# A perceiver layer on one core: the first context group turned block by block while x is normalised, and the last two places run one token tile after the other

## The chip, the core and the metric

The kernel runs on one core of a Trainium2 chip. The metric is the device time of one execution in microseconds, as the median of several runs. TensorE (PE in the profile, with its weight loads as PEld) multiplies and transposes; it takes its operands from SBUF and writes into the eight banks of PSUM, each 128 partitions by 512 float32 numbers. VectorE (DVE) and ScalarE (ACT) read those banks and write SBUF. GpSimd (POOL) has a small part. Transfers from and to memory are issued by the queue of SyncE (SP) or of ScalarE and run on sixteen shared DMA engines. All data are float32.

## The reference

A batch of one: 256 tokens `x` of 512 channels, and a context of 25088 rows of 512 channels. Three residual parts follow one another.

```python
x = x + xattn(layernorm(x), ctx, ctx)   # qp = q Wq + bq, kp = k Wk + bk (128 wide), vp = v Wv + bv
                                        # sigmoid(qp kp^T / sqrt(128)) @ vp, no softmax
x = x + attn(layernorm(x))              # 16 heads of 64, one shared key and value head, causal softmax,
                                        # projection, layernorm of the result
x = x + ffn(layernorm(x))               # 64 experts of width 256, the best 8 for each token,
                                        # and a shared expert of width 1024 behind a sigmoid gate
```

## The kernel before

**The cross attention** takes most of the time. The 25088 rows are cut into 49 groups of 512 rows (four blocks of 128). For a group the kernel needs the context turned (channels on the partitions, `cT`), the keys (`keys`, line 339: four chunks of 128 channels summed into one PSUM bank, then a DVE copy with the bias, `kT`), the scores (`scores`, line 360: two banks, each of two blocks by 256 queries, then ACT's sigmoid into `zT`), and the sum of context rows weighted by the scores (`values`, line 432, in seven products instead of eight, from sums and differences that DVE prepares in `query_sums` and `context_sums`). Those products stay in four PSUM banks (`xacc`, pool `pacc`, tag `acc`) over all groups. From the third group on the context is turned by DVE from a second load of it (`quarters`); the first two groups are turned by TensorE (`turn_by_pe`, line 320: chunk after chunk, four transposes into one bank, and a copy of the bank to SBUF by DVE or ACT in turn).

**PSUM.** Four banks are the accumulators. The other four are shared by everything else in this stage: `bank` (line 80) gives every fourth request the one bank called `apart`, and the other requests one of three under the tag `one`. A request has to wait until the bank's last user has been copied out. After the cross attention the accumulators make place for two pairs of banks (`banks`, line 580).

**The start.** bk and bq are loaded by ACT's queue. SP's queue issues, in this order, the two tiles of x (256 KB each), wqT, the first context group in four parts of 256 KB, the plain key weights (256 KB), the second group (1 MB in one), the key weights in another order (four parts), and the quarters of the third group. TensorE first runs idle matmuls (`keep_warm(4)`, line 457). DVE and ACT normalise x tile by tile (`layernorm`: `bn_stats`, `bn_aggr`, a square root on ACT, a reciprocal and one scaling). TensorE then transposes x into `xnT` (`transposed`, line 300, copied by DVE), turns group 0, makes the queries (`pq`, then `qT` with its bias), the keys of group 0, turns group 1, and enters the loop over the groups. Instructions inside `in_turn` keep the program's order on their engine; the others are placed by the framework's own scheduler. All the matmuls of this stage and nearly all of DVE's work are pinned so.

**The end.** In the expert part, eight places are run whole, one expert each: `gate_up` makes the hidden tile `hT` for all 256 tokens, `down` (line 977) multiplies it with the down weights for each of the two token tiles and adds the weighted result to `y`. `run` (line 1000) lets `gate_up` of the next place go ahead of `down` of the one before. Seven more experts with few tokens are computed in between in 32-row quarters; their results in `of_sb` are spread over the tokens by `few_spread` (line 1246: for each token tile three products, added to `y`). It stands behind the `down` of the last but one place. After the last `down` both token tiles of `y` are stored by SP (`store`, line 1275). Then a count read from memory decides whether further experts remain, which here is a branch not taken.

Of the kernel before, what the change touches and what calls it, by code (L numbers as in the profile page):

```python
# [9 lines left out]
F32 = mybir.dt.float32  # L10
AF = mybir.ActivationFunctionType
ALU = mybir.AluOpType
AX = mybir.AxisListType

P = 128
# [6 lines left out]
def tile_perceiver_layer(  # L22
# [25 lines left out]
    nc = tc.nc  # L48

    T, D = x.shape  # L50
    S = context.shape[0]
    QK = wqT.shape[1]
# [6 lines left out]
    NT = T // P  # L59
    ND = D // P  # L60
    NI = I // P
    J = 4
# [11 lines left out]
    cpool = cross.enter_context(tc.tile_pool(name="cpool", bufs=2))  # L74
# [15 lines left out]
    pacc = cross.enter_context(tc.tile_pool(name="pacc", bufs=4, space=bass.MemoryType.PSUM))  # L90

    def load(name, shape, src, pool=const):
        t = pool.tile(shape, F32, tag=name, name=name, bufs=1)
        nc.sync.dma_start(t, src)
        return t

    def rows(src):
        return src.rearrange("(c p) f -> p c f", p=P)  # L100
# [25 lines left out]


    BY_PE = 2
    bk_sb = const.tile([QK, 1], F32, tag="bk", name="bk")
    nc.scalar.dma_start(bk_sb, bk)  # L130
    bq_sb = const.tile([QK, 1], F32, tag="bq", name="bq")
    nc.scalar.dma_start(bq_sb, bq)
    x_sb = act.tile([P, NT, D], F32, tag="x", name="x_sb")
    for t in range(NT):
        nc.sync.dma_start(x_sb[:, t, :], x[t * P : (t + 1) * P, :])
    wqT_sb = load("wqT", [P, ND, QK], rows(wqT))
    load_context(0, parts=J)
    wk_plain_sb = load("wk_plain", [P, ND, QK], rows(wkT), cpool)
    load_context(1)
    wkT_sb = const.tile([P, ND, QK], F32, tag="wkT", name="wkT_sb")  # L140
    for a in range(NA):
# [52 lines left out]
    ident = const.tile([P, P], F32, tag="ident", name="ident")  # L194
# [41 lines left out]
    def keep_warm(n):  # L236
        pi = bank("pi")
        for _ in range(n):
            nc.tensor.matmul(pi, lhsT=idle_sb[:, 0:P], rhs=idle_sb, start=True, stop=True)
# [20 lines left out]
    def layernorm(dst, src, nm, twice=False):  # L260

        mean, sd, rs = moments(src, nm, twice)
        in_turn(nc.vector.reciprocal(rs, sd))
        in_turn(nc.vector.tensor_scalar(dst, src, mean, rs, ALU.subtract, ALU.mult))
# [32 lines left out]
                    )  # L297
                )

    def transposed(dst, src, nm):  # L300

        for c in range(ND):
            pt = bank(f"pt_{nm}_{c}")
            for t in range(NT):
                nc.tensor.transpose(
                    pt[:, t * P : (t + 1) * P], src[:, t, c * P : (c + 1) * P], ident
                )
            nc.vector.tensor_copy(dst[:, c, :], pt[:, :T])


    turned_tiles = {}

# [4 lines left out]
        in_turn(nc.vector.transpose(cT, q.rearrange("p b (c r) -> p c b r", r=R)))  # L317
        turned_tiles[g] = cT

    def turn_by_pe(g):  # L320

        cT = cpool.tile([P, ND, J * P // R, R], F32, tag="cT", name=f"cT_{g}")
        ct = ctx_tiles[g]
        for c in range(ND):
            pt = bank(f"ptc_{g}_{c}")
            for j in range(J):
                in_turn(
                    nc.tensor.transpose(
                        pt[:, j * P : (j + 1) * P], ct[:, j, c * P : (c + 1) * P], ident
                    )  # L330
                )
            to = cT[:, c, :, :].rearrange("p b r -> p (b r)")
            if c % 2:
                nc.scalar.copy(to, pt)
            else:
                in_turn(nc.vector.tensor_copy(to, pt))
        turned_tiles[g] = cT

    def keys(g):

        cT = turned_tiles.pop(g)
        pk = bank(f"pk_{g}")
        w = wk_plain_sb if g < BY_PE else wkT_sb
        for c in range(ND):
            in_turn(
                nc.tensor.matmul(  # L346
                    pk,
                    lhsT=w[:, c, :],
                    rhs=cT[:, c, :, :].rearrange("p b r -> p (b r)"),
                    start=(c == 0),  # L350
                    stop=(c == ND - 1),
                )
            )
        kT = cpool.tile([QK, J * P], F32, tag="kT", name=f"kT_{g}")
        in_turn(nc.vector.tensor_scalar(kT, pk, bk_sb, None, ALU.add))  # L355
        return kT
# [38 lines left out]
    NP = J // 2  # L395
    HD = D // 2
    product = {}
    for i, names in enumerate((("00", "01"), ("2", "3"), ("1",), ("4", "11"))):
        held = pacc.tile([P, 512], F32, tag="acc", name=f"xacc_{i}")
        for k, nm in enumerate(names):  # L400
            product[nm] = held[:, k * HD : (k + 1) * HD]
    sums, channel_sums = {}, {}

    def z_of(zT, i, b):
# [49 lines left out]
                    )  # L454
                )

    keep_warm(4)
    xn = work.tile([P, NT, D], F32, tag="tok", name="xn")
    for t in range(NT):
        layernorm(xn[:, t, :], x_sb[:, t, :], f"x{t}")  # L460
    xnT = work.tile([P, ND, T], F32, tag="tokT", name="xnT")
    transposed(xnT, xn, "xn")
    turn_by_pe(0)
    pq = bank("pq")
    for c in range(ND):
        in_turn(
            nc.tensor.matmul(
                pq[:, :T],
                lhsT=wqT_sb[:, c, :],
                rhs=xnT[:, c, :],  # L470
                start=(c == 0),
                stop=(c == ND - 1),
            )
        )
    qT = cpool.tile([QK, T], F32, tag="qT", name="qT", bufs=1)
    in_turn(nc.vector.tensor_scalar(qT, pq[:, :T], bq_sb, None, ALU.add))
# [103 lines left out]
    def banks(name):  # L580
        return pairs.tile([P, 2, 512], F32, tag="two", name=name)
# [392 lines left out]

    y = late.tile([P, NT, D], F32, tag="y", name="y")

    def down(n, hT):
        _, dn = weights.pop(n)
        nm = f"{n[0]}{n[1]}"
        for t in range(NT):  # L980
            pd = banks(f"pd_{nm}_{t}")[:, 0, :]
            for f in range(NI):
                nc.tensor.matmul(  # L983
                    pd,
                    lhsT=hT[:, f, t * P : (t + 1) * P],
                    rhs=dn[:, f, :],
                    start=(f == 0),
                    stop=(f == NI - 1),
                )
            w = wsh[:, t, :] if n[0] == "s" else wso[:, t, n[1] : n[1] + 1]  # L990
            if n == ("s", 0):
                nc.vector.scalar_tensor_tensor(
                    y[:, t, :], pd, w, x2[:, t, :], ALU.mult, ALU.add
                )
            else:
                nc.vector.scalar_tensor_tensor(
                    y[:, t, :], pd, w, y[:, t, :], ALU.mult, ALU.add
                )

    def run(names, between):  # L1000

        pending = None
        for i, n in enumerate(names):
            hT = gate_up(n, first if n == ("s", 0) else None)
            if pending is not None:
                down(*pending)
            pending = (n, hT)
            if i in between:
                between[i]()
        down(*pending)  # L1010
# [232 lines left out]
                )  # L1243
        nc.scalar.copy(of_sb[:, r, :], po)

    def few_spread():
        for t in range(NT):
            pd = banks(f"pd_few_{t}")[:, 0, :]
            for r in range(NR):
# [7 lines left out]
            nc.vector.tensor_add(y[:, t, :], pd, y[:, t, :])  # L1257

    def places(lo, hi, also=()):
# [10 lines left out]
        run(  # L1270
            [("e", k) for k in range(lo, hi)],
            {i: (lambda fs=fs: [f() for f in fs]) for i, fs in between.items()},
        )

    def store():
        for t in range(NT):
            nc.sync.dma_start(out[t * P : (t + 1) * P, :], y[:, t, :])

    def remaining(lo):

# [3 lines left out]
        with tc.If(n_left > lo):  # L1284
# [93 lines left out]
```

## Time and profile before

| | us |
|---|---|
| median of three runs (797.99 to 798.13) | 798.07 |
| profiled execution, its own time | 798.27 |
| its span in the profile | 796.4 |
| TensorE busy within the span | 784.4 |
| first transpose of x starts / second tile's six go on | 7.87 / 8.39 |
| first matmul of the queries | 11.04 |
| first matmul of the scores of group 0 | 18.02 |
| first matmul of the keys of group 1 | 19.74 |
| last matmul done, start of the last sum | 790.02 |
| second half of the output: store issued | 790.8 |

The profile is of one execution. Its times are microseconds from the start of the span; a matmul in float32 is two instructions of TensorE, a transpose one. A line of the timeline gives the start, the time covered, the engine, the line of the program, the operation and its tiles, the count, and in brackets the idle time before it with what ended it. A line of the chain of waits gives start, duration and the work that the end of the span was waiting for.

### The profile page before, as it was taken

How to read it: one execution, taken by the hardware profiler on the slowest of the kernel's cores; microseconds unless marked ns; L12 is line 12 of the kernel's file. 1: busy time of each engine (PE TensorE's matmuls, PEld its weight loads, DVE VectorE, ACT ScalarE, POOL GpSimd, SP SyncE). 2: the span in 40 equal slices, each digit the busy share in tenths (PEclk: the TensorE clock that was granted, in tenths of full speed). 3: DMA queues.
4: the chain of work that ended last, by engine and by line, in shares of the span. 5: the costliest groups of instructions: out<-in, count | busy, mean ns of one | idle time of the engine just before them, and what ended most of it. 6: DMA issues, size and time to landing. Idle time of an engine off the chain costs nothing.

```text
span 796.4 us, 8701 instructions
## 1 busy us (share of the span) xinstructions
PE 784.4 (98%) x3298; PEld 564.5 (71%) x3298; DVE 496.6 (62%) x820; ACT 112.3 (14%) x248; POOL 21.4 (3%) x44
## 2 busy tenths in 40 slices
PE   9999999999999999999999999999999899999996
PEld 5777777777777777777777777777676586776563
DVE  5766776677766776677766776676656563512222
ACT  2111101110011101110011101110245220110110
POOL 1000000000000000000000000000223000000000
PEclk9999999999999999999999999999999999999998
DMA  9967998999887778777887778720510042769400
GB/s 279 257 165 185 258 243 242 244 248 242 200 205 185 174 176 209 191 184 170 197 206 184 174 177 211 193 72 0 196 44 1 1 133 96 252 233 392 163 1 30
DMA packets 150497, 139.59 MB, mean 175 GB/s; under 512 B 7984, under 2 KB 109872, under 8 KB 150448
## 3 DMA queue, kind: packets, MB, share of 16 engines
q1 hardware_dynamic: 150160, 138.96, 67.1%
q8 instruction: 28, 0.46, 0.3%
q14 instruction: 21, 0.17, 0.1%
q10 hardware_dynamic: 288, 0.00, 0.0%
HBM read 138.42 MB, written 0.52 MB: 174 GB/s over the span
## 4 chain that ended last, share of the span: by engine, by line
PE 96%; DVE 2%; ACT 1%; DMA 0%; POOL 0%; issue 0%; ACTq 0%
PE xacc L448 37%; PE pk L346 21%; PE pz L368 11%; PE ph_e L936 7%; PE pd_e L983 3%; PE ph_s L936 3%; PE pd_s L983 2%; PE pa L651 2%; PE ph_few L1205 1%; PE pw L715 1%; PE py L564 1%; PE ps L741 1%; PE ptp L792 1%; PE po_few L1236 1%; PE pf L1182 1%; PE pd_few L1250 1%
## 5 line engine op out<-in xcount | busy, mean ns | idle before, releaser
L346 PE MATMUL pk<-cT,wkT_sb 128*128 128x512 f32 x376 | 169.0, 592 | 0.0
L448 PE MATMUL xacc<-T,S 128*128 128x256 f32 x588 | 134.9, 379 | 0.0
L376 ACT ACTIVATE zT<-pz 128x512 f32<-128x512 f32 x98 | 58.3, 597 | 479.9 <-PE pz L368 479.2
L448 PEld LDWEIGHTS xacc<-T,S 128*128 128x128 f32 x588 | 111.7, 190 | 15.2
L346 PEld LDWEIGHTS pk<-cT,wkT_sb 128*128 128x128 f32 x376 | 71.4, 190 | 69.9 <-issue 67.4
L317 DVE STREAM_TRANSPOSE cT<-quarters 128x2048 f32<-128x2048 f32 x47 | 108.3, 2304 | 0.0
L448 PEld LDWEIGHTS xacc<-ctx,zT 128*128 128x128 f32 x392 | 74.3, 190 | 31.3 <-issue 23.0
L448 PE MATMUL xacc<-ctx,zT 128*128 128x256 f32 x392 | 93.0, 380 | 0.1
L368 PE MATMUL pz<-qT,kT 128*128 128x256 f32 x392 | 92.6, 379 | 0.0
L368 PEld LDWEIGHTS pz<-qT,kT 128*128 128x128 f32 x392 | 74.4, 190 | 10.1
L416 DVE TENSOR_TENSOR S<-zT 128x256 f32<-128x256 f32 x49 | 20.8, 425 | 91.4 <-ACT zT L376 91.4
L355 DVE TENSOR_SCALAR kT<-pk,bk 128x512 f32<-128x512 f32 x49 | 36.8, 751 | 59.8 <-PE pk L346 59.8
L936 PE MATMUL ph_e<-fT,gu 128*128 128x256 f32 x256 | 57.4, 381 | 0.0
L388 DVE TENSOR_TENSOR zsum<-zsum,zT 128x1024 f32<-128x1024 f32 x48 | 56.8, 1184 | 0.0
L936 PEld LDWEIGHTS ph_e<-fT,gu 128*128 128x128 f32 x256 | 48.0, 190 | 10.6 <-issue 2.2
L448 PE MATMUL xacc<-T,zT 128*128 128x256 f32 x196 | 50.3, 379 | 0.0
L448 PE MATMUL xacc<-ctx,S 128*128 128x256 f32 x196 | 50.3, 379 | 0.0
L448 PEld LDWEIGHTS xacc<-T,zT 128*128 128x128 f32 x196 | 37.2, 190 | 5.1
L448 PEld LDWEIGHTS xacc<-ctx,S 128*128 128x128 f32 x196 | 37.2, 190 | 5.1
L427 DVE TENSOR_TENSOR T<-ctx,T 128x512 f32<-128x512 f32 x49 | 33.9, 692 | 1.7
L428 DVE TENSOR_TENSOR T<-ctx 128x512 f32<-128x512 f32 x49 | 33.5, 685 | 0.0
L429 DVE TENSOR_TENSOR T<-T,ctx 128x512 f32<-128x512 f32 x49 | 33.5, 684 | 0.0
(231 smaller groups left out, 611.3 us busy)
## 6 DMA issues: line engine op xcount, KB each, us to landing
ctx<-in_context SPq DMA_DIRECT2D x48, 1024.0 KB, 6.5
quarters<-in_context SPq DMA_DIRECT2D x188, 256.0 KB, 8.4
gu<-in_e_gate_up SPq DMA_DIRECT2D x12, 1024.0 KB, 7.5
dn<-in_e_down SPq DMA_DIRECT2D x11, 512.0 KB, 4.7
gu_s<-in_s_gate_up SPq DMA_DIRECT2D x8, 512.0 KB, 5.9
a_wqT<-in_a_wqT SPq DMA_DIRECT2D x1, 2048.0 KB, 8.8
a_wout<-in_a_woutT SPq DMA_DIRECT2D x1, 2048.0 KB, 9.9
dn_s<-in_s_down SPq DMA_DIRECT2D x4, 512.0 KB, 7.2
```

The source lines that it names most:

```text
L317: in_turn(nc.vector.transpose(cT, q.rearrange("p b (c r) -> p c b r", r=R)))
L346: nc.tensor.matmul(pk, lhsT=w[:, c, :], rhs=cT[:, c, :, :].rearrange("p b r -> p (b r)"), start=(c == 0), stop=(c == ND - 1),)
L355: in_turn(nc.vector.tensor_scalar(kT, pk, bk_sb, None, ALU.add))
L368: nc.tensor.matmul(pz[:, i * T : (i + 1) * T], lhsT=kT[:, j * P : (j + 1) * P], rhs=qT, start=True, stop=True,)
L376: nc.scalar.activation(zT[:, 2 * h : 2 * h + 2, :].rearrange("p j t -> p (j t)"), pz, AF.Sigmoid, scale=1.0 / math.sqrt(QK),)
L388: in_turn(nc.vector.tensor_add(zsum, zsum, zT))
L427: in_turn(nc.vector.tensor_sub(t2, c_of(ct, 1, 1), t1))
L428: in_turn(nc.vector.tensor_sub(t3, c_of(ct, 1, 1), c_of(ct, 0, 1)))
L429: in_turn(nc.vector.tensor_sub(t4, t2, c_of(ct, 1, 0)))
L448: nc.tensor.matmul(product[nm], lhsT=lhs[:, p, :], rhs=rhs[:, p, :], start=(g == 0 and p == 0 and nm in ("00", "2", "1", "4")), stop=(g == ...
L936: nc.tensor.matmul(ph[:, f * T + lo : f * T + hi], lhsT=gu[:, c, col : col + P], rhs=fT[:, c, lo:hi], start=(c == 0), stop=(c == ND - 1),)
L983: nc.tensor.matmul(pd, lhsT=hT[:, f, t * P : (t + 1) * P], rhs=dn[:, f, :], start=(f == 0), stop=(f == NI - 1),)
```

## The change

1. **Loads.** `x`'s two tiles go out on two queues, the first on SP's and the second on ACT's. SP continues with the four blocks of context group 0; ACT's queue takes the plain key weights and then wqT; bk and bq follow on SP behind the context blocks. The rest of the order stays.
2. **x.** Two idle matmul pairs instead of four. The moments of both token tiles are taken first, then both are scaled. The transposes of x go into four shared banks, taken one after the other, and are copied by ACT (even chunks) and DVE (odd chunks) instead of by DVE alone.
3. **Group 0** is turned block by block (each block's four channel chunks go to four banks), into the four accumulator banks, which are handed to the accumulators afterwards (`open_products`). The order on TensorE is blocks 0, 1, 2, x tile 0, block 3, x tile 1. All the copies come after the last block, ACT taking the even chunks and DVE the odd ones.
4. **Queries** are made in the middle of the keys of group 0: chunks 0 and 1 of the keys, the four of the queries, chunks 2 and 3 of the keys. `context_sums(0)` follows the keys instead of coming before them.
5. **Group 1** is turned block by block as well, into the four shared banks.
6. **The end.** `few_spread` and `down` are cut into functions of one token tile. The last two places run, for token tile 0: few-seat spread, last but one `down`, last `down`, store; then the same for token tile 1, whose last `down`, sum and store are in two halves of 256 channels.

```diff
-    def load(name, shape, src, pool=const):
+    def load(name, shape, src, pool=const, queue=nc.sync):
         t = pool.tile(shape, F32, tag=name, name=name, bufs=1)
-        nc.sync.dma_start(t, src)
+        queue.dma_start(t, src)
...
-    bk_sb = const.tile([QK, 1], F32, tag="bk", name="bk")
-    nc.scalar.dma_start(bk_sb, bk)
-    bq_sb = const.tile([QK, 1], F32, tag="bq", name="bq")
-    nc.scalar.dma_start(bq_sb, bq)
     x_sb = act.tile([P, NT, D], F32, tag="x", name="x_sb")
-    for t in range(NT):
-        nc.sync.dma_start(x_sb[:, t, :], x[t * P : (t + 1) * P, :])
-    wqT_sb = load("wqT", [P, ND, QK], rows(wqT))
+    for t, queue in enumerate((nc.sync, nc.scalar)):
+        queue.dma_start(x_sb[:, t, :], x[t * P : (t + 1) * P, :])
     load_context(0, parts=J)
-    wk_plain_sb = load("wk_plain", [P, ND, QK], rows(wkT), cpool)
+    wk_plain_sb = load("wk_plain", [P, ND, QK], rows(wkT), cpool, nc.scalar)
+    wqT_sb = load("wqT", [P, ND, QK], rows(wqT), queue=nc.scalar)
+    bk_sb = load("bk", [QK, 1], bk)
+    bq_sb = load("bq", [QK, 1], bq)
     load_context(1)
...
-    def turn_by_pe(g):
+    def turned_by_pe(g, where):
         cT = cpool.tile([P, ND, J * P // R, R], F32, tag="cT", name=f"cT_{g}")
+        turned_tiles[g] = cT
         ct = ctx_tiles[g]
-        for c in range(ND):
-            pt = bank(f"ptc_{g}_{c}")
-            for j in range(J):
+        pts = [where(f"ptc_{g}_{c}") for c in range(ND)]
+        for j in range(J):
+            for c in range(ND):
                 in_turn(
                     nc.tensor.transpose(
-                        pt[:, j * P : (j + 1) * P], ct[:, j, c * P : (c + 1) * P], ident
+                        pts[c][:, j * P : (j + 1) * P], ct[:, j, c * P : (c + 1) * P], ident
                     )
                 )
+            yield
+        for c in range(ND):
             to = cT[:, c, :, :].rearrange("p b r -> p (b r)")
             if c % 2:
-                nc.scalar.copy(to, pt)
+                in_turn(nc.vector.tensor_copy(to, pts[c]))
             else:
-                in_turn(nc.vector.tensor_copy(to, pt))
-        turned_tiles[g] = cT
-
-    def keys(g):
+                in_turn(nc.scalar.copy(to, pts[c]))
+        yield
+
+    def keys(g, between=None):
...
         for c in range(ND):
+            if between is not None and c == ND // 2:
+                between()
...
-    keep_warm(4)
+    keep_warm(2)
     xn = work.tile([P, NT, D], F32, tag="tok", name="xn")
-    for t in range(NT):
-        layernorm(xn[:, t, :], x_sb[:, t, :], f"x{t}")
+    found = [moments(x_sb[:, t, :], f"x{t}") for t in range(NT)]
+    for t, (mean, sd, rs) in enumerate(found):
+        in_turn(nc.vector.reciprocal(rs, sd))
+        in_turn(nc.vector.tensor_scalar(xn[:, t, :], x_sb[:, t, :], mean, rs, ...))
     xnT = work.tile([P, ND, T], F32, tag="tokT", name="xnT")
-    transposed(xnT, xn, "xn")
-    turn_by_pe(0)
-    pq = bank("pq")
...
+    pxs = [bank(f"pt_xn_{c}") for c in range(ND)]
+
+    def turn_x(t):
+        for c in range(ND):
+            in_turn(nc.tensor.transpose(pxs[c][:, t * P : (t + 1) * P], xn[:, t, c * P : (c + 1) * P], ident))
+
+    blocks = turned_by_pe(0, sum_bank)
+    for j in range(J - 1):
+        next(blocks)
+    turn_x(0)
+    next(blocks)
+    turn_x(1)
+    next(blocks)
+    open_products()
+    for c in range(ND):
+        if c % 2:
+            in_turn(nc.vector.tensor_copy(xnT[:, c, :], pxs[c][:, :T]))
+        else:
+            in_turn(nc.scalar.copy(xnT[:, c, :], pxs[c][:, :T]))
...
+    kT = keys(0, first_queries)
     context_sums(0)
-    kT = keys(0)
-    turn_by_pe(1)
+    for _ in turned_by_pe(1, bank):
+        pass
...
-    def few_spread():
-        for t in range(NT):
-            pd = banks(f"pd_few_{t}")[:, 0, :]
+    def few_spread(t):
+        pd = bank(f"pd_few_{t}")
...
+    def by_tiles(last_but_one, last):
+        for t in range(NT):
+            few_spread(t)
+            down_tile(*last_but_one, t, mark=in_turn)
+            for lo, hi in ((0, D),) if t == 0 else ((0, D // 2), (D // 2, D)):
+                down_tile(*last, t, lo, hi, mark=in_turn)
+                store_tile(t, lo, hi)
+        weights.pop(last_but_one[0])
+        weights.pop(last[0])
...
-            (7, few_spread),
         ],
+        by_tiles,
     )
...
-    store()
```

`sum_bank(name)` takes one bank of the pool `pacc`. `down_tile(n, hT, t, lo, hi, where, mark)` is the body of the old `down` for one token tile and the channels `lo` to `hi`, in a bank of the pairs. `run` hands the last two places to `last_downs`, here `by_tiles`, once the last `gate_up` is issued.

More of the change, by code (lines that the diff above doesn't have):

```diff
@@ L298, in transposed_tile @@
                 )
-    def transposed(dst, src, nm):
-        for c in range(ND):
-            pt = bank(f"pt_{nm}_{c}")
-            for t in range(NT):
[L305 to L308, printed above, removed]
     turned_tiles = {}
@@ L318, in turn @@
         turned_tiles[g] = cT
-    def turn_by_pe(g):
+    def turned_by_pe(g, where):
         cT = cpool.tile([P, ND, J * P // R, R], F32, tag="cT", name=f"cT_{g}")
+        turned_tiles[g] = cT
         ct = ctx_tiles[g]
-        for c in range(ND):
-            pt = bank(f"ptc_{g}_{c}")
-            for j in range(J):
+        pts = [where(f"ptc_{g}_{c}") for c in range(ND)]
+        for j in range(J):
+            for c in range(ND):
                 in_turn(
                     nc.tensor.transpose(
-                        pt[:, j * P : (j + 1) * P], ct[:, j, c * P : (c + 1) * P], ident
+                        pts[c][:, j * P : (j + 1) * P], ct[:, j, c * P : (c + 1) * P], ident
                     )
                 )
+            yield
+        for c in range(ND):
             to = cT[:, c, :, :].rearrange("p b r -> p (b r)")
             if c % 2:
-                nc.scalar.copy(to, pt)
+                in_turn(nc.vector.tensor_copy(to, pts[c]))
             else:
-                in_turn(nc.vector.tensor_copy(to, pt))
-        turned_tiles[g] = cT
-    def keys(g):
+                in_turn(nc.scalar.copy(to, pts[c]))
+        yield
+    def keys(g, between=None):
         cT = turned_tiles.pop(g)
@@ L397, in tile_perceiver_layer, with sum_bank, open_products @@
     product = {}
[L398 to L401, printed above, removed]
+    def sum_bank(name):
+        return pacc.tile([P, 512], F32, tag="acc", name=name)
+    def open_products():
+        for i, names in enumerate((("00", "01"), ("2", "3"), ("1",), ("4", "11"))):
+            held = sum_bank(f"xacc_{i}")
+            for k, nm in enumerate(names):
+                product[nm] = held[:, k * HD : (k + 1) * HD]
     sums, channel_sums = {}, {}
@@ L455, in values @@
                 )
-    keep_warm(4)
+    keep_warm(2)
     xn = work.tile([P, NT, D], F32, tag="tok", name="xn")
-    for t in range(NT):
-        layernorm(xn[:, t, :], x_sb[:, t, :], f"x{t}")
-    xnT = work.tile([P, ND, T], F32, tag="tokT", name="xnT")
-    transposed(xnT, xn, "xn")
-    turn_by_pe(0)
-    pq = bank("pq")
-    for c in range(ND):
-        in_turn(
[L467 to L472, printed above, removed]
-            )
-        )
@@ L475, in tile_perceiver_layer @@
-    qT = cpool.tile([QK, T], F32, tag="qT", name="qT", bufs=1)
-    in_turn(nc.vector.tensor_scalar(qT, pq[:, :T], bq_sb, None, ALU.add))
+    found = [moments(x_sb[:, t, :], f"x{t}") for t in range(NT)]
+    for t, (mean, sd, rs) in enumerate(found):
+        in_turn(nc.vector.reciprocal(rs, sd))
+        in_turn(
+            nc.vector.tensor_scalar(
+                xn[:, t, :], x_sb[:, t, :], mean, rs, ALU.subtract, ALU.mult
+            )
+        )
+    xnT = work.tile([P, ND, T], F32, tag="tokT", name="xnT")
@@ new lines, in tile_perceiver_layer @@
+    pxs = [bank(f"pt_xn_{c}") for c in range(ND)]
+    def turn_x(t):
+        for c in range(ND):
+            in_turn(
+                nc.tensor.transpose(
+                    pxs[c][:, t * P : (t + 1) * P], xn[:, t, c * P : (c + 1) * P], ident
+                )
+            )
+    blocks = turned_by_pe(0, sum_bank)
[11 more added lines that the diff above has]
+            in_turn(nc.scalar.copy(xnT[:, c, :], pxs[c][:, :T]))
@@ new lines, in tile_perceiver_layer, with first_queries @@
+    qT = cpool.tile([QK, T], F32, tag="qT", name="qT", bufs=1)
+    def first_queries():
+        pq = bank("pq")
+        for c in range(ND):
+            in_turn(
+                nc.tensor.matmul(
+                    pq[:, :T],
+                    lhsT=wqT_sb[:, c, :],
+                    rhs=xnT[:, c, :],
+                    start=(c == 0),
+                    stop=(c == ND - 1),
+                )
+            )
+        in_turn(nc.vector.tensor_scalar(qT, pq[:, :T], bq_sb, None, ALU.add))
@@ L975, in tile_perceiver_layer, with down_tile @@
     y = late.tile([P, NT, D], F32, tag="y", name="y")
[L977 to L982, printed above, removed]
+    def down_tile(n, hT, t, lo=0, hi=D, where=None, mark=lambda ins: ins):
+        dn = weights[n][1]
+        nm = f"pd_{n[0]}{n[1]}_{t}_{lo}"
+        pd = where(nm) if where is not None else banks(nm)[:, 0, :]
+        for f in range(NI):
+            mark(
                 nc.tensor.matmul(
-                    pd,
+                    pd[:, lo:hi],
                     lhsT=hT[:, f, t * P : (t + 1) * P],
-                    rhs=dn[:, f, :],
+                    rhs=dn[:, f, lo:hi],
                     start=(f == 0),
@@ L989, in down, with run @@
                 )
[L990 to L1000, printed above, removed]
+            )
+        w = wsh[:, t, :] if n[0] == "s" else wso[:, t, n[1] : n[1] + 1]
+        onto = x2 if n == ("s", 0) else y
+        nc.vector.scalar_tensor_tensor(
+            y[:, t, lo:hi], pd[:, lo:hi], w, onto[:, t, lo:hi], ALU.mult, ALU.add
+        )
+    def down(n, hT):
+        for t in range(NT):
+            down_tile(n, hT, t)
+        weights.pop(n)
+    def run(names, between, last_downs=None):
         pending = None
@@ L1004, in run @@
             hT = gate_up(n, first if n == ("s", 0) else None)
+            if last_downs is not None and i == len(names) - 1:
+                return last_downs(pending, (n, hT))
             if pending is not None:
@@ L1244, in few_down @@
         nc.scalar.copy(of_sb[:, r, :], po)
-    def few_spread():
-        for t in range(NT):
-            pd = banks(f"pd_few_{t}")[:, 0, :]
-            for r in range(NR):
+    def few_spread(t):
+        pd = bank(f"pd_few_{t}")
+        for r in range(NR):
+            in_turn(
                 nc.tensor.matmul(
@@ L1256, in few_spread, with places @@
                 )
-            nc.vector.tensor_add(y[:, t, :], pd, y[:, t, :])
-    def places(lo, hi, also=()):
+            )
+        nc.vector.tensor_add(y[:, t, :], pd, y[:, t, :])
+    def places(lo, hi, also=(), last_downs=None):
         between = {}
@@ L1272, in places, with store_tile @@
             {i: (lambda fs=fs: [f() for f in fs]) for i, fs in between.items()},
+            last_downs,
         )
+    def store_tile(t, lo=0, hi=D):
+        nc.sync.dma_start(out[t * P : (t + 1) * P, lo:hi], y[:, t, lo:hi])
     def store():
         for t in range(NT):
-            nc.sync.dma_start(out[t * P : (t + 1) * P, :], y[:, t, :])
+            store_tile(t)
+    def by_tiles(last_but_one, last):
+        for t in range(NT):
+            few_spread(t)
[5 more added lines that the diff above has]
+        weights.pop(last[0])
     def remaining(lo):
```

## The prediction

> **What bounds the kernel now.** I read the page first: is there one engine that is never idle?
>
> ```profile
> span 796.4 us, 8701 instructions
> PE 784.4 (98%) x3298; PEld 564.5 (71%) x3298; DVE 496.6 (62%) x820; ACT 112.3 (14%) x248; POOL 21.4 (3%) x44
> PE 96%; DVE 2%; ACT 1%; DMA 0%; POOL 0%; issue 0%; ACTq 0%
> ```
>
> TensorE is. So the change can gain only at the two ends, where something else is last, and it loses wherever it opens a hole in TensorE's row. For the front I read the chain of waits in order of time (start us, us, what):
>
> ```profile
> 0.76 3.61 DMA x_sb<-in_x
> ...
> 7.79 0.56 DVE xn L264
> 8.35 0.04 issue
> 8.39 0.88 PE pt_xn L305 x6
> 9.27 1.94 PE ptc L328 x16
> 11.20 1.80 PE pq L467 x8
> 13.00 3.43 PE pk L346 x8
> 16.43 1.75 PE ptc L328 x16
> 18.18 1.73 PE pz L368 x8
> 19.91 3.43 PE pk L346 x8
> ```
>
> Up to 8.39 the chain is x landing and being normalised; from there TensorE runs without a hole. By the timeline's starts the blocks begin at 11.04 (queries), 16.27 (second transposes), 18.02 (scores) and 19.74 (second keys); queries with first keys take 16.27 - 11.04 = 5.23 us. Then the timeline of the front (start, duration, engine, line, what):
>
> ```profile
> 1.60 6.43 PE L239 MATMUL pi<-idle_sb 128*128 128x512 f32 x8 [1.60 <-DVE idle_sb L234]
> 2.14 2.75 SPq L124 DMA_DIRECT2D ctx<-in_context  x4
> 9.23 1.97 PE L328 MATMUL ptc<-ident,ctx 128*128 128x128 f32 x16
> 16.47 0.75 DVE L355 TENSOR_SCALAR kT<-pk,bk 128x512 f32<-128x512 f32 x1 [0.42 <-PE pk L346]
> 18.82 1.28 ACT L376 ACT_TABLE_LOAD   x1
> ```
>
> The eight idle matmuls start 0.855 us apart, while a keys matmul of the same shape takes 3.43 / 8 = 0.43: TensorE is at half speed until about 7.1, though the clock column grants 1.00 from the start. And, from the waits of the queues (waiting, for whom, us in total, times, longest), why the fourth context block is issued only near 4.5:
>
> ```profile
> SPq L124 <- DMA bk<-in_bk: 1.0, 1, 1.0
> ```
>
> The ninth transfer waits for the first to land. At the end, by the chain and then by the timeline:
>
> ```profile
> 786.57 3.45 PE pd_e L983 x8
> 790.02 0.03 issue
> 790.04 0.75 DVE y L996
> ```
>
> ```profile
> 789.10 2.29 SPq L1277 DMA_DIRECT2D out<-y  x2
> ```
>
> After TensorE come one 0.75 us sum, a store of 256 KB (3.0 to 3.4 us to land), and some 2.2 us to the span's end.
>
> **The queues.** The second x tile, the key weights and the query weights leave SP for ACT: three issues of 0.40 to 0.46 us. ACT's table load at 1.68 then runs some 0.45 us later, to 3.4; the first square root needs it at 5.3, so nothing is paid (if x landed 1.9 us sooner, 0.45 would be). bk and bq move behind the context blocks on SP; they land near 9, needed at 14 and 16. With bk and bq out of the first eight, no context block waits for a landing: issued at 1.2, 1.6, 2.05 and 2.5. The first, as before 4.5 us in flight, lands at 5.8 (before 6.6). The fourth is bounded by that row at 7.0, and by bytes at 9.2: before, 1.83 MB (the one-microsecond windows added up) had moved some 0.6 us ahead of its landing at 8.5, and now up to 0.5 MB of weights in 512-byte rows share the way (403 GB/s in 8.39 to 11.04, 252 after, when such rows mix in). I take 8.5. ctx_1, wkT and the quarters follow on SP within about 1.5 us of their old times; ctx_1 landed at 12.1 and is wanted after 15, the quarters by 22 and wanted at 26.6: hidden.
>
> The Trainium skill, "DMA: Bandwidth & Descriptors", section "Rules for kernel authors", speaks against this part: spreading transfers over SP and ACT brings no bandwidth, only sequencer time, since both run on the same engines. By the rule the fourth block would stay at its 8.5, by the issue row it would come at 7.0; the sum below stands on neither.
>
> **Normalising x.** Both moments come first: statistics 4.39 to 5.09 and 5.3 to 6.0, aggregates 0.19 each, then reciprocal 0.17 and xn 0.55 twice. xn of tile 0 is ready at 6.95 (was 6.41), of tile 1 at 7.7 (was 8.35).
>
> **First transposes.** Two idle matmul pairs instead of four end near 5.2, two microseconds before full speed came. A transpose takes 1.75 / 16 = 0.11 us at full speed, so 0.214 at half. From 5.8, at half speed, blocks 0 to 2 and x tile 0 (16 transposes, 3.42) end at 9.2, whichever time the fourth block takes up to there. Block 3's first transpose ends at 9.4, ACT sees it at 9.6. Now a wait takes the place of the removed one: all four shared PSUM banks hold x, so the first keys cannot open a bank until ACT has copied context chunk 0 (0.59), chunk 2 (0.59) and x chunk 0 (0.37), to 11.15. Queries and keys start then instead of at 11.04: **+0.1**. The 2.65 us of transposes in front of them do leave the chain, but wait, half speed and copies fill the place. The accumulators' banks, which hold the first transposes, are free from 11 and wanted at 22: hidden. At full speed the fourth block's landing rules: block 3 at 8.6, start near 10.4, **-0.65**; with the block at 7.0, xn and four transposes rule (7.4), start 9.2, **-1.85**.
>
> **Keys around queries.** Same 16 instructions, 5.23 us; end E. The second context differences move behind the key copy on DVE (below).
>
> **Second transposes, block by block.** Before, chunk after chunk: a bank was wanted every 0.44 us. Now four banks are wanted at once and the first keys hold one of the four. The key copy runs from E + 0.20 to E + 0.95 (16.47 against 16.27 before). TensorE stops after three transposes, at E + 0.33, until E + 1.0: **+0.67**. The other thirteen end at E + 2.43. Every copy can start only in the last block: ACT's chunk 0 runs from E + 2.3 to E + 2.9, and the scores' first bank is chunk 0's: **+0.52**. On DVE the four context differences (2.6 us from E + 0.9) now stand before chunks 1 and 3, which are copied by E + 4.2 and E + 4.8. The second score bank is one of the other three: free at E + 3.5 if ACT's chunk 2 hands it over, no wait (half of the scores last until E + 3.8), at E + 4.25 if it must be DVE's chunk 1, **+0.45**. I take 0, since DVE's is not needed where any will do, and keep 0.45. Second keys at E + 4.67 against E + 3.47: **+1.2**. The sigmoid behind ACT's table load is ready by E + 6.0, before the keys end at E + 8.1: hidden.
>
> **The end.** The few-seat sum moves from behind the last but one place's sums to between them, and from the paired banks to a shared one last used before 778.7. The same columns pass TensorE: 12 few-seat products and 16 whole ones, of which 8 are split into 16 of 256 columns (0.216 each, as in the scores). The spread's sources were copied at 772.4, the last hidden tile was ready at 778.7; they are wanted at 778 and 782: hidden. Tile 0's store leaves some 5 us early, beside matmuls. The last half opens the bank of the product before it: its sum ends 0.95 + 0.05 after that product, the first half is done after 0.865: +0.13. The last sum has 256 columns: 0.43 (the nearest 128x256 row) for 0.75: -0.32. The last store is 128 KB: at the 400 GB/s seen 0.33 less, at a fixed cost 0; I take -0.25. A third issue on SP (0.37 to 0.57) ends before the last sum does. Together **-0.44**, bounds +0.1 (fixed store cost, issues colliding) and -0.65.
>
> **Sum.** +0.1 + 1.2 - 0.44 = +0.86 on the profiled execution's 798.27, which is 0.20 above the median; on the median 798.07 that makes 798.9.
>
> **Rivals.**
>
> *Slower: the clock stays low into the first keys.* Before, full speed took 5.5 us of unbroken work; now the work breaks at 5.2, resumes at 5.8 and breaks again before the keys at 11.15. Each microsecond of keys and queries at half speed costs half of it, up to 5.2 us for all. It decides from about 0.75 / 0.5 = 1.5 us of half speed past 11.15, that is full speed only after 12.65. Three microseconds give 798.9 + 1.5 = 800.4. Against it: 5.8 to 10.9 is 5.1 us of nearly unbroken work. The Trainium skill, "TensorE: Matmul & The Clock Gate", section "Part 1: The HAM clock gate", wants one busy window of about 3.4 us, free-running; the row shows 5.5 from the start of work, which a window starting 2 us late would give. By the page full speed comes by 10.5 and this rival costs nothing.
>
> *Faster: the clock is up by 7.1 as before* (the pause in the idle matmuls is short) and the blocks land early. Front -0.65 to -1.85, waits +1.2, end -0.44: +0.1 to -1.1, 798.2 to 797.0. More than 0.2% (1.6 us) needs x itself to land 0.5 us sooner as well: 796.3.
>
> *The waits do not come:* only the front and the end change, -0.35, or 797.7. Against it: four banks and five tiles that want one.
>
> **How the numbers follow.** About 0.2%, 1.6 us, is what a measurement of this kernel can tell from no change. Half speed until about 10.5, as summed (+0.4 to +1.6 with both bank cases): 0.45. Clock up early: 0.25, of which 0.05 is beyond -1.6. Low clock into the keys, or the fourth block later than 10 as well: 0.22, beyond +1.6. No waits or a size misread: 0.08, of which 0.05 faster by more than 1.6. So faster 0.10, same 0.68, slower 0.22. The range runs from the early clock with early blocks, -1.1 (797.0), to three microseconds of low clock with the 0.45 of the second bank (800.9).
>
> **What would show it.** Right: transposes 0.21 us apart up to about 10; the first keys released by ACT's xnT copy; TensorE idle 0.7 us before the second group's transposes go on, released by kT, and again 0.5 us before the scores, released by ACT's cT; last sum 0.43 long, TensorE ending 0.1 to 1.4 us later than 790.02. Wrong: no hole in TensorE between 11 and 21; full speed before 8; first keys before 9.5 or after 12; or a changed spacing in the long loop, which I take as untouched.

## The result, and the profile after

The changed kernel takes 799.46 us (median of 20 executions, 799.21 to 800.67) and the kernel before 798.10 in the same sessions (797.90 to 798.32): 1.36 us more, a ratio of 1.0020 (95% interval 1.0013 to 1.0027). Against the bound of 0.2% that is "no change", right at its edge on the slow side. The 20 executions do not scatter evenly: 14 lie between 799.21 and 799.61 and six between 800.15 and 800.67. The profiled one is of the upper group (800.38, span 798.5), so its lines show about 1.1 us more than a usual execution.

The page first: TensorE's busy time is what it was, to the digit, and the span has grown by 2.1 us. The loss is idle time.

```profile
span 798.5 us, 8704 instructions
PE 784.4 (98%) x3298; PEld 565.1 (71%) x3298; DVE 495.8 (62%) x819; ACT 112.6 (14%) x250; POOL 21.4 (3%) x44
```

The chain of waits at the front (start us, us, what), to be held against the one before the change:

```profile
2.13 6.04 DMA ctx<-in_context
...
8.22 0.73 PE ptc L318 x4
8.95 0.85 PE pt_xn L474 x4
9.80 0.85 PE ptc L318 x4
10.66 0.85 PE pt_xn L474 x4
11.51 2.22 PE pk L340 x4
13.73 1.73 PE pq L498 x8
15.46 1.73 PE pk L340 x4
...
17.21 0.76 DVE kT L349
...
18.02 1.32 PE ptc L318 x10
...
19.37 0.59 ACT cT L328
...
20.01 1.99 PE pz L362 x8
22.00 3.43 PE pk L340 x8
```

Three things are new. The chain begins with a context block's landing (6.04 us) instead of x's. Four transposes take 0.85 us, twice the 0.44 of full speed. And after the first keys two entries stand that are not TensorE's: the key copy on DVE and the copy of the second group on ACT. By the timeline's starts the blocks stand at 11.46 (first keys; before, queries at 11.04), 17.01 (second transposes; 16.27), 20.01 (scores; 18.02) and 21.84 (second keys; 19.74). So 0.42 us are lost up to the first keys, 0.32 within them, 1.25 in the second transposes, 0.11 in the scores: 2.10, the whole growth of the span.

The low clock has its own column. In one-microsecond windows (stretch, length, then the busy time of PE, PEld, DVE, ACT, POOL with the count of instructions, then the granted clock, the DMA share and GB/s):

```profile
7.00:8.00 1.00, 0.50 (x4) 0.26 (x3) 0.56 (x2) 0.00 (x0) 0.00 (x0) 1.00 1.05 400
8.00:9.00 1.00, 0.78 (x6) 0.79 (x7) 0.00 (x0) 0.00 (x0) 0.00 (x0) 0.83 1.11 366
9.00:10.00 1.00, 1.00 (x6) 1.00 (x5) 0.00 (x0) 0.00 (x0) 0.00 (x0) 0.50 1.06 412
11.00:12.00 1.00, 1.00 (x4) 0.61 (x3) 1.00 (x3) 0.71 (x3) 0.00 (x0) 0.50 1.15 222
12.00:13.00 1.00, 1.00 (x3) 0.38 (x2) 0.22 (x1) 0.00 (x0) 0.00 (x0) 0.96 0.99 202
```

TensorE waits for blocks between 6 and 8, its clock is halved during the ninth microsecond, and full speed is back at 12, in the middle of the first keys. The whole executions agree: their mean granted clock is 0.997 for the six of the upper group and 0.998 for the fourteen of the lower.

The two holes, in the timeline (its brackets are shorter than the holes, since a transpose is drawn to its modelled end and not to the start of the next):

```profile
18.02 1.64 PE L318 MATMUL ptc<-ident,ctx 128*128 128x128 f32 x13 [0.52 <-DVE kT L349]
20.01 1.99 PE L362 MATMUL pz<-qT,kT 128*128 128x256 f32 x8 [0.35 <-ACT cT L328]
```

At the end, the chain and below it the last sums in the timeline:

```profile
788.67 3.71 PE pd_e L1016 x12
792.38 0.02 issue
792.40 0.48 DVE y L1026
```

```profile
791.23 0.73 PEld L1016 LDWEIGHTS pd_e<-dn,hT_e 128*128 128x128 f32 x4 [0.38 <-DVE y L1026]
792.40 0.48 DVE L1026 SCALAR_TENSOR_TENSOR y<-pd_e,wso,y 128x256 f32<-128x256 f32 x1 [0.63 <-PE pd_e L1016]
```

The last sum is 0.48 us long instead of 0.75, but the last half product waits for a sum (0.38 before its weight load), and the last products take 3.71 us for 3.45. The last sum ends at 792.88, 2.09 us later than the 790.79 of before: the end neither gains nor loses. From there to the end of the span it is 5.62 us, as before (5.61), although the last store has half the bytes.

### The profile page after: what moved, and what is told of

The parts are those of the page before. It is cut to its first block, busy times and chain, and to the rows that moved or that the text cites. A ratio compares the mean times of both kernels' runs of the same rounds, so it can differ in the third digit from the quotient of the medians.

```text
span 798.5 us, 8704 instructions
## 1 busy us (share of the span) xinstructions
PE 784.4 (98%) x3298; PEld 565.1 (71%) x3298; DVE 495.8 (62%) x819; ACT 112.6 (14%) x250; POOL 21.4 (3%) x44
## 4 chain that ended last, share of the span: by engine, by line
PE 95%; DVE 2%; DMA 1%; ACT 1%; POOL 0%; issue 0%; SPq 0%; ACTq 0%
PE xacc L448 37%; PE pk L340 21%; PE pz L362 11%; PE ph_e L968 7%; PE pd_e L1016 4%; PE ph_s L968 3%; PE pd_s L1016 2%; PE pa L683 2%; PE ph_few L1243 1%; PE pw L747 1%; PE py L596 1%; PE ps L773 1%; DMA ctx<-in_context 1%; PE ptp L824 1%; PE po_few L1274 1%; PE pf L1220 1%
```

## The experiments

The kernel before ran beside each group of runs; its medians there were 797.91 (first four runs), 797.99 (the other seven). Times below are medians of 10 or 11 executions.

### The two halves of the change

`front_only` has the changed start and the old end (parts 1 to 5 of the change); `end_only` the reverse (part 6). The diff is that of the change, cut in two.

> The start of the changed kernel with the end of the kernel before. Theory: the whole loss is in the start (two new holes in TensorE of 0.7 and 0.6 us before and after the second group's transposes, and a low clock at the first transposes in some executions), and the end is worth nothing. Then this takes the changed kernel's time, about 1.3 us above the kernel before (799.4), again in two groups of executions some 1.1 us apart. Rival, from the prediction's own sum: the end is worth -0.44, so that without it the time is 1.7 to 1.8 above the kernel before (799.9).

> The start of the kernel before with the end of the changed kernel. Theory: the shorter last sum (-0.27) is eaten by the wait of the last half for its bank (+0.26), and a store of half the size lands no sooner: 798.1, within 0.1 of the kernel before, in one group. Rival, from the prediction's sum: 0.44 faster, 797.7.

`front_only` took 799.52 us, 1.61 above the kernel beside it (ratio 1.0023, 1.0014 to 1.0033), with eight executions at 799.42 to 799.71 and two at 800.5 and 800.6. `end_only` took 798.18 (1.0003, 0.9994 to 1.0012). So the loss is in the start, and the end is worth nothing that can be measured. The two together make 1.88, 0.52 more than the changed kernel's 1.36; the intervals (1.1 to 2.6 and -0.5 to 1.0 us) hold that, and the kernel before was itself 0.19 faster beside these runs. The interval of `end_only` just holds the forecast -0.44 as well, so it is the trace that decides. The chain of `end_only` shows how its gain is lost:

```profile
786.49 3.71 PE pd_e L984 x12
...
790.22 0.48 DVE y L994
```

Last sum done at 790.70 for 790.79: a sum 0.27 us shorter, 0.26 us of waiting for the paired bank. The last store has half the bytes and lands no sooner. Its row, first in the kernel before and then in `end_only` (KB, us from issue to landing):

```profile
out<-y SPq DMA_DIRECT2D x1, 256.0 KB, 3.0
```

```profile
out<-y SPq DMA_DIRECT2D x1, 128.0 KB, 2.9
```

In the changed kernel the last half took 3.3 us. The end of the span does not follow the landing closely either: in `front_only` a last store of 256 KB landed in 2.4 us, and the span ended 5.67 us after the last sum, against 5.6 in the other three. What is last there the traces do not name, and I left it open.

The profile of `front_only` fell in the lower group, and so shows the same start without the low clock (chain of waits):

```profile
8.80 0.44 PE pt_xn L474 x4
9.23 0.12 PE ptc L318
...
9.38 1.07 ACT cT L328 x2
10.46 0.28 ACT xnT L491
...
10.78 1.98 PE pk L340 x4
```

Transposes of four take 0.44, the clock column stays at 1.00, and the first keys start at 10.78, 0.26 earlier than the queries did before. They are released by ACT's copy of x, the third of its copies: TensorE has nothing to do from about 9.95, when the second x tile is transposed, to 10.78. The second keys start at 20.87, 1.13 later than before: the holes behind the first keys cost 1.24 here as well (16.05 to 19.04, for 1.75 before).

### The holes behind the first keys

```diff
-    kT = keys(0, first_queries)
     context_sums(0)
-    for _ in turned_by_pe(1, bank):
-        pass
+    kT = keys(0, first_queries)
+    turn_by_chunks(1)        # chunk after chunk, as before the change
```

> The changed kernel with group 1 turned chunk after chunk again, and its first context differences before the first keys, as before the change. Theory: the holes behind the first keys go (0.7 for the key copy, 0.6 for ACT's copy of the second group), so 1.2 to 1.4 us less than the changed kernel: 798.1 (fast group) and 799.2 (slow group), and no idle time of TensorE between the first keys and the scores. Rival: the start is held by something behind the holes (the sigmoid's table load, DVE's copies), which then takes their place: 799.0 or more.

It took 798.16 us (1.0003, 0.9994 to 1.0012), 1.36 less than `front_only` beside it, which has the old end, and 1.30 less than the changed kernel. The slow group expected near 799.2 did not appear: the eleven executions lie between 797.78 and 798.90. The chain after the first keys is whole again:

```profile
14.55 1.72 PE pk L359 x4
16.27 1.75 PE ptc L339 x16
18.01 1.73 PE pz L381 x8
19.74 3.43 PE pk L359 x8
```

Against the same chain before the change (16.43, 18.18 and 19.91) the blocks begin 0.16 to 0.17 us sooner. So the block order of the second group, with its four banks wanted at once, is what costs the 1.2 to 1.3 us; of the rest of the new start some 0.2 us is left in this trace at full clock, and nothing in the time. The run moves the context differences too. They hold neither hole: in the changed kernel's lines the releasers are `kT` and ACT's `cT`, and the differences run on DVE only behind the key copy.

### The clock

Two ways to fill the pauses of TensorE. `kept_busy` puts idle matmuls of 256 and 128 columns behind each of the first two context blocks; `kw3` keeps three idle pairs instead of two.

```diff
     for j in range(J - 1):
         next(blocks)
+        if j < 2:
+            for n in (256, 128):
+                in_turn(nc.tensor.matmul(pxs[0][:, T : T + n], lhsT=idle_sb[:, 0:P],
+                                         rhs=idle_sb[:, 0:n], start=True, stop=True))
```

```diff
-    keep_warm(2)
+    keep_warm(3)
```

> The changed kernel with two small idle matmuls (384 columns together, 0.65 us at full speed) after each of the first two context blocks, into columns of a bank that x doesn't use. Theory: the second group of executions comes from TensorE's clock going down after idle pauses between the blocks, at a time that differs from run to run; with the pauses filled all executions are at full clock, one group near 799.3, spread below 0.6. Rival: the slow group comes from context blocks that land late; then two groups 1.1 apart remain, and the fillers cost up to 0.2.

> The changed kernel with three idle matmul pairs instead of two, so that the pause of TensorE between them and the second context block is filled. Theory: the slow group of executions (1.1 us longer, about a third of them) comes from the clock going down after the pauses; here nearly all executions are in the faster group, 1.2 to 1.4 above the kernel before, none more than 1.8 above. Rival: the slow group comes from elsewhere and stays at a third.

`kw3` took 799.45 us, all eleven executions between 799.20 and 799.61: the upper group is gone, at no cost to the lower. That is the expected reading; with six upper executions in 20, chance alone would give it about once in fifty times. Together with the 0.50 in the clock column it makes the low clock the cause of the changed kernel's upper group, of which there is one trace. The pauses shrink but do not go. First the changed kernel's second and third block, then those of `kw3`:

```profile
6.84 0.66 PE L318 MATMUL ptc<-ident,ctx 128*128 128x128 f32 x4 [0.76 <-DMA ctx<-in_context]
8.22 0.73 PE L318 MATMUL ptc<-ident,ctx 128*128 128x128 f32 x4 [0.72 <-DMA ctx<-in_context]
```

```profile
7.04 0.66 PE L318 MATMUL ptc<-ident,ctx 128*128 128x128 f32 x4 [0.60 <-DMA ctx<-in_context]
8.23 0.66 PE L318 MATMUL ptc<-ident,ctx 128*128 128x128 f32 x4 [0.53 <-DMA ctx<-in_context]
```

`kept_busy` missed its expectation: 799.55, eleven executions spread from 798.9 to 800.1 in no two groups. In its profile the first block and the first fillers ran at half speed, since the clock had not come up yet when the two idle pairs ended, and so the fillers themselves held the next blocks:

```profile
5.56 1.08 PE ptc L318 x4
6.65 1.14 PE pt_xn L485 x4
7.79 0.44 PE ptc L318 x4
```

Its clock column reads 1.00 through the whole start, so the spread of this run stays unexplained.

### The two queues, and the bank that x holds

`one_queue` has the changed order of loads with every load on SP. `x_two_banks` puts the transposes of x in two banks instead of four.

```diff
-    for t, queue in enumerate((nc.sync, nc.scalar)):
+    for t, queue in enumerate((nc.sync, nc.sync)):
...
-    wk_plain_sb = load("wk_plain", [P, ND, QK], rows(wkT), cpool, nc.scalar)
-    wqT_sb = load("wqT", [P, ND, QK], rows(wqT), queue=nc.scalar)
+    wk_plain_sb = load("wk_plain", [P, ND, QK], rows(wkT), cpool)
+    wqT_sb = load("wqT", [P, ND, QK], rows(wqT))
```

> The changed kernel with all loads on SP again, in the changed order (both x tiles, the four context blocks, the key weights, wqT, bk, bq). Theory: the weights on the second queue share the way with the context blocks and make the later ones late (blocks 2 and 3 took 5.1 to 6.2 us to land, instead of 4.5), and their landing holds the first transposes. On one queue the blocks land near 5.8, 6.3, 6.8 and 7.3; the first keys start near 9.3 instead of 10.8 at full clock: 1.0 to 1.5 us less than the changed kernel, about 0 to 0.3 above the kernel before. Rival: the same bytes take the same way in any order, block 3 lands near 8.5 as before the change: no gain, 1.3 above the kernel before.

```diff
-    pxs = [bank(f"pt_xn_{c}") for c in range(ND)]
+    pxs = [bank(f"pt_xn_{c}") for c in range(ND // 2)]      # two chunks of 256 columns in each
+    turns[0] += 2                                            # the later requests get the banks they got before
...
+    for h, copy in enumerate((nc.scalar.copy, nc.vector.tensor_copy)):
+        in_turn(copy(xnT[:, 2 * h : 2 * h + 2, :].rearrange("p c t -> p (c t)"), pxs[h]))
```

> The changed kernel with the transposes of x in two shared banks (two chunks of 256 columns in each, copied by one ACT and one DVE instruction) instead of four, so that a bank is free for the first keys. Theory: the first keys wait for no copy of x, only for the first copy of the context: they start 0.8 us earlier (near 10.0 at full clock), released by ACT's cT; 0.7 to 0.8 us less than the changed kernel, 0.5 to 0.6 above the kernel before. Rival: the copies of the other context chunks or the key weights' landing hold them as long: less than 0.2 gained.

`one_queue` took 798.79 us (1.0016, 1.0007 to 1.0025): seven executions at 798.45 to 798.87 and four at 799.87 to 800.33. The middle of the seven, 798.67, is 0.78 below the 799.45 of `kw3` in the same session, less than expected; its first keys start at 9.76, 1.02 earlier than in `front_only`. The granted clock of the four upper executions is 0.998 and 0.999, like that of the other seven, so here the low clock is not shown as their cause. The rows of transfers (KB each, median us from issue to landing), first of the changed kernel and then of `one_queue`:

```profile
ctx<-in_context SPq DMA_DIRECT2D x4, 256.0 KB, 5.6
x_sb<-in_x ACTq DMA_DIRECT2D x1, 256.0 KB, 4.0
x_sb<-in_x SPq DMA_DIRECT2D x1, 256.0 KB, 3.8
wk_plain<-in_wkT ACTq DMA_DIRECT2D x1, 256.0 KB, 4.9
```

```profile
ctx<-in_context SPq DMA_DIRECT2D x4, 256.0 KB, 4.3
x_sb<-in_x SPq DMA_DIRECT2D x2, 256.0 KB, 2.8
wk_plain<-in_wkT SPq DMA_DIRECT2D x1, 256.0 KB, 5.0
```

The context blocks land 1.3 us sooner after their issue, and x 1.0 to 1.2 sooner. The run changes two things for the blocks: the queue, and the place of the weights, which now come behind them. What each is worth to the blocks it can't tell; for x the next run does.

`x_two_banks` took 798.99 (1.0017, 1.0008 to 1.0026), seven executions at 798.74 to 799.07 and four at 799.83 to 800.55, with 798.83 in the middle of the seven, 0.62 below `kw3`; its first keys start at 9.97, right behind the last transposes, 0.81 earlier than in `front_only`. The wait for the bank was there and goes; of its 0.81 us the time shows three quarters.

### x and the second queue alone

The kernel before, with bk and bq taken from ACT's queue and put behind the key weights on SP; nothing else.

```diff
-    bk_sb = const.tile([QK, 1], F32, tag="bk", name="bk")
-    nc.scalar.dma_start(bk_sb, bk)
...
     wk_plain_sb = load("wk_plain", [P, ND, QK], rows(wkT), cpool)
+    bk_sb = load("bk", [QK, 1], bk)
+    bq_sb = load("bq", [QK, 1], bq)
```

> The kernel before with one edit: bk and bq leave ACT's queue and are loaded by SP behind the plain key weights. Theory: with a second queue issuing in the first microsecond (bk and bq before the change, x, key weights and wqT after it) the first x tile takes 3.6 to 4.0 us to land, with SP alone 2.7 to 2.8; so x lands near 3.5 here, the second x tile is ready before the idle matmuls end at 8.0, and TensorE goes on without its wait at 8.39: 0.3 to 0.45 us less than the kernel before. Rival: x landed sooner with SP alone only because the weights had left its way; then x lands near 4.3 here as well, and the time stays within 0.1.

It took 797.64 us; the kernel before 797.99 beside it (ratio of all 0.9998, 0.9989 to 1.0007, in which one execution at 799.94 weighs). The median gains the expected 0.35, within an interval that can't tell it from nothing. That x lands sooner is plain in its chain, against `0.76 3.61` before:

```profile
0.75 2.85 DMA x_sb<-in_x
```

Two transfers of 512 bytes on a second queue had held x's 256 KB by 0.76 us. The other traces agree: the x rows have a median of 2.7 to 3.0 us in the five kernels where SP alone loads in the first microsecond, and 3.7 to 4.2 where ACT's queue does too. TensorE's wait for the second x tile did not go, as the expectation had it: the idle matmuls ended sooner as well, and it waits 0.65 us, until 7.63 instead of 8.39. Why a second queue that starts in the first microsecond delays the first queue's transfers, the traces do not show.

### Together

`all_three` has one queue, x in two banks and the second group by chunks, with the two idle pairs of the change; `all_three_kw3` has three pairs; `all_three_kw3_end` also gives the last half product a bank of the shared ones:

```diff
-                down_tile(*last, t, lo, hi, mark=in_turn)
+                down_tile(*last, t, lo, hi, bank if lo else None, in_turn)
```

> One queue, x in two banks, and group 1 chunk after chunk with its context differences early, all on the changed kernel. Theory: the gains add where the chain runs through each: first keys near 8.6 at full clock, and no holes behind them: 2.0 to 2.5 us faster than the kernel before (795.5 to 796.0) at full clock, 0.5 to 1.0 faster in executions with a low clock at the transposes. Rival: the context blocks don't land sooner on one queue; then the first keys start near 10.0, 0.8 to 1.0 faster than the kernel before.

> The kernel with one queue, x in two banks and group 1 by chunks, with three idle matmul pairs instead of two. Theory: the wide spread of that kernel (796.65 to 799.3) is the clock going down in the pauses before the context blocks, at a phase that differs between executions; with three pairs the executions come together within 0.6 us, between 796.7 and 797.3, about 1.0 us (0.13%) faster than the kernel before. Rival: the spread is of the landing times on one queue; then it stays above 1.5 us.

> The same with the last half product in one of the shared banks, so that it doesn't wait for a paired bank. Theory: the wait of 0.26 us at the last half goes and the last sum stays at 0.48: 0.2 to 0.3 us less than with the wait, and TensorE runs without a hole to its end. Rival: something else holds the last half, no gain.

`all_three` took 798.40 us, spread from 796.65 to 799.3: three executions, at 796.65 to 796.87, are where the gains of the single runs add up (799.45 less 0.78, 0.62 and 1.36 is 796.69). Even these are 1.1 to 1.3 us faster than the kernel before, and not the expected 2.0 to 2.5. Its profile is of one of them, with first keys at 9.33 instead of 8.6. The others may pay for a low clock, but that is not shown: there is no trace of one, and their granted clocks (0.995 to 0.999) do not set them apart. With three pairs the executions come together at 797.13 (796.36 to 797.69), ratio 0.9988 (0.9979 to 0.9997) to the kernel before. TensorE's chain has no entry of another engine from 1.59 on:

```profile
1.59 5.49 PE pi L237 x6
7.08 1.50 PE ptc L318 x12
...
9.46 0.44 PE pt_xn L494 x4
9.90 1.90 PE pk L359 x4
```

The spread, 1.3 us, is wider than the 0.6 expected. With the free bank at the end it is 797.00 (796.08 to 797.81), ratio 0.9986 (0.9977 to 0.9995): the last products take 3.46 instead of 3.71, so the wait goes as expected, but the 0.13 us between the medians lie within both spreads. In its profile the second transposes wait for the landing of the second group, until 15.41, which is 5.49 us behind the first keys instead of 5.26: the loads may be part of the spread that is left. Both versions are about 1 us faster than the kernel before (0.86 and 0.99), and so 2.2 to 2.35 faster than the changed one.

## Why the prediction was right

The forecast was 798.9 us, no change by the 0.2% bound, with a range of 797.0 to 800.9; 799.46 was measured. The ledger, step by step.

- **First keys' start, +0.1 forecast.** The measured starts are 11.46 with the low clock (+0.42) and 10.78 at full clock (-0.26). The mechanism I named, a bank that x holds until ACT's third copy, is what releases the keys, and `x_two_banks` removes it. The path up to there was wrong in its parts. I had TensorE bound by half speed from 5.8 on; in fact the context blocks bound it, landing near 5.3, 6.8, 8.2 and 8.8 where I had 5.8 for the first and 8.5 for the last, and in the profile of the lower group all transposes but the first four ran at full clock. So one of my own signs of being wrong came, full speed before 8, and the sign of being right, transposes 0.21 us apart up to 10, came only in the upper group, where the clock had fallen again.
- **Key copy, +0.67 forecast.** TensorE pauses from 17.34 to 18.02, 0.68.
- **ACT's copy before the scores, +0.52 forecast.** With the key copy's wait it makes 1.19; the second transposes took 1.25 longer. `group1_by_chunks` took both away and with them 1.30 to 1.36 us.
- **The second score bank, 0 taken and 0.45 kept.** The scores took 0.11 longer. TensorE waited there for ACT's `cT` and for no copy of DVE, so the 0.45 did not come.
- **The end, -0.44 forecast.** This is the step that failed: 0.0 in the trace and +0.27, within its interval, in `end_only`. The last sum's -0.32 was -0.27; the bank's +0.13 was +0.26; and the store's -0.25 was nothing, since 128 KB took 2.9 and 3.3 us to land where the last 256 KB had taken 3.0. That fits the fixed cost I had kept only as a bound. (Of the two stores before, the last is the one of 3.0 us, so 2.6 us lay behind its landing and not 2.2.) With the end at nothing the sum is +1.3, close to the measured 1.36, but not term by term: in the trace at full clock it is -0.26 up to the first keys, +0.04 in them, +1.24 in the second transposes and +0.11 in the scores, 1.13 in all, where I had +0.1 and +1.2.
- **The loop** keeps its spacing: 11.2 us from the second group's scores to the third's in both traces.
- **The rival of the low clock** was placed on the right resource with the wrong story. I saw the clock as still coming up when the keys start; it had come up and went down again, after pauses of 0.7 us. It takes about 1.1 us in 6 of 20 executions. The page "TensorE: Matmul & The Clock Gate" of the Trainium skill, section "Part 1: The HAM clock gate", has a free-running window of about 3.4 us, which the low stretch from 8.7 to 12.0 and its absence in other executions agree with. By the same section the clock goes down after at least one idle window of this length; the trace has none before 8.7, its longest pause is 0.76 us, and the measurement decides.
- **The rule against the second queue** (the Trainium skill, "DMA: Bandwidth & Descriptors", "Rules for kernel authors": no bandwidth, only sequencer time) held in its direction; the rows go further, a loss of a microsecond for x, and of 1.3 for the blocks in the run that moved the weights as well. I had used neither in the sum, and the blocks' landing was in fact on the chain.

The holes are shown by their removal, the low clock by its column and by `kw3`. That the total came out so near is partly luck, two misses of opposite sign: the end, 0.44 too good, and the way to the first keys, 0.36 too bad for the usual executions.

## What to carry to other kernels

Before you turn a loop around so that it wants several PSUM banks at once, count the banks and ask who holds each when the loop begins: here four wanted banks out of four cost 1.25 us in waits, while the old order asked for one at a time. Where idle matmuls keep TensorE's clock up, take too many rather than too few: here pauses of 0.7 us between blocks lost the clock in some executions and not in others, and a third pair ended that at no cost. And try issuing a transfer that has to land first without a second queue beside it: here x gained 0.76 us.

## What was not expected of the hardware

- The clock fell without any long idle stretch: TensorE was busy 24% and 50% of the two microseconds from 6 to 8, with no pause over 0.8 us, and the grant went from 1.00 to 0.50 for 8.7 to 12.0.
- The clock column reads 1.00 from the start although the first idle matmuls run at half speed; worked out from their spacing, full speed came near 7.1 in the profile before and near 5 in `before_biases_late` (eight idle matmuls took 6.43 us and 5.16).
- A second queue issuing in the first microsecond, even two transfers of 512 bytes, delayed the first tile of x from 2.85 us to 3.61.
- A last store of half the bytes landed no sooner: 128 KB in 2.9 and 3.3 us, 256 KB in 3.0 and, in `front_only`, 2.4.
